# A first transformer with its own attention class: shifted rows by DMA, two scalings on ScalarE, query lengths on the score rows, narrow products in one run

## Chip, cores and metric

One core of one Trainium2 chip runs the whole program. The metric is the device time of one execution in microseconds (us); the time before is the median of three runs. TensorE (PE; its weight loads are shown as PEld), VectorE (DVE), ScalarE (ACT), GpSimd (POOL) and the queue of SyncE (SP), which issues most of the DMAs, each take their instructions in the order in which the program lists them. That order comes from a scheduler at build time, which places the instructions that the Python generators emit.

## The reference, cut to what matters

The program is a chain of four blocks on 4 x 512 tokens of width 128 (the kernel's layout), each an attention-like part times the SiLU of a feed-forward-like part. The change touches the "feed-forward" of the third block, which is itself a transformer of 6 layers with 16 heads of 64 and a window of 32:

```python
def shift_tokens(t):              # the second half of the columns comes from the token before
    a, s = jnp.split(t, 2, -1)
    s = jnp.pad(s, ((0, 0), (1, 0), (0, 0)))[:, :-1]
    return jnp.concatenate([a, s], -1)
def attn_layer(x, Wqkv, qs, ksc, Wo):
    q, k, v = heads of (x @ Wqkv)
    q = l2norm(q) * qs            # unit length, then a learned scale
    k = l2norm(k) * ksc
    q = q * cos * scale + rotate_half(q) * sin * scale
    k = k * cos * inv + rotate_half(k) * sin * inv
    ...
    sim = einsum('bhwie,bhwje->bhwij', bq, bk2) * 8.0     # own window and the one before, masked
    out = softmax(sim) @ bv2
    return out @ Wo
def ffn_layer(x, g, bln, W1, b1, W2, b2):
    xn = layernorm(x) * g + bln
    a, gate = jnp.split(xn @ W1 + b1, 2, -1)
    return a * gelu(gate) @ W2 + b2
for i in range(6):
    x = attn_layer(shift_tokens(x), ...) + x
    x = ffn_layer(shift_tokens(x), ...) + x
```

The fourth block has a second transformer (2 layers, 8 heads, window 64) that shares some of the code.

## The kernel before

`transformer` (L707) builds one `_Transformer` for each of the two and runs three generators side by side: `queries_keys`, `attention` and `feed_forward`. Work goes by rows (layer, batch entry), 24 of them in the first transformer, and each row has two slots (`gp`, eight heads each), so 48 slots. In a slot `merge` takes the next piece of the generator that is least far along; the `yield` values are the planned TensorE times. All TensorE results go through one pool of four PSUM tiles of two banks (`S2`, printed as S).

- `queries_keys` (L1278). The shifted row `hb` is made by two DVE copies and a memset (`shifted`, L84 to L91). For queries (i = 0), then keys (i = 1), two groups g: two 128x512 products into one S tile (projections `hb,l_wqk`), their squares on ACT (L1304), the two halves added on POOL (L1305), two products with the rotary table on DVE (L1306, L1308), their sum on POOL (L1309). `unit_length` (L1319) sums the squares over each head with two products against ones, takes Ln and Exp on ACT (L1329, L1330) and scales the rotated tile on DVE (L1333); eight DMAs (L1340) then stack it by heads into `l_qk`. `tables` (L1250) loads a rotary table by DMA once per layer and kind and scales it on DVE (L1258).
- `attention` (L1495). A unit is half a slot (`j`). `scores` (L1383): two masks as products with an identity, 64 narrow products (64 rows x 32 columns), the transposes of the last unit (`turn`, L1431) in their middle, then on DVE the row maxima (L1415), the subtraction in two halves (L1419), the exponential on ACT (L1424), the sums on DVE (L1426). `turn_back` (L1484) transposes the unit before that, `wo` is multiplied (L1532), the row `xn` updated (L1533). `weigh` (L1443): 64 narrow products of the last unit in two pieces, then the division on DVE (L1473). `values` (L1343): products 128x64 by 256 columns in two pieces, an eviction each (L1365), four DMAs into the buffer `l_ve` with the keys' windows one step on.
- `feed_forward` (L1543). Shift by DVE again, mean and variance by two products, the normalised row on DVE (L1558) and its gain and offset on DVE (L1559), three pairs of products with W1, GELU on ACT (L1569), the product on DVE (L1571), three with W2, the update (L1579). The second transformer runs the same function.

Of the kernel before, what the change touches and what calls it, by code (L numbers as in the profile page):

```python
# [38 lines left out]
class Net:  # L39
# [667 lines left out]
    def transformer(self, pre, depth, heads, window, consts):  # L707

        with ExitStack() as stack:
            pool = lambda name, bufs=1, **kw: stack.enter_context(self.pool(pre + name, bufs, **kw))
            pools = [pool("ps", 4, space=PSUM)]

            pools += [pool("c", side="right"), pool("tab", 3, side="right"), pool("w", side="right")]
            pools += [pool("qk", 4), pool("v", 2), pool("p", 2), pool("t", 2)]
            t = _Transformer(self, pre, heads, window, pools, consts)
            t.exp_tables()  # L720
            rows = [(l, b) for l in range(depth) for b in range(B)]
            passes = t.queries_keys(rows), t.attention(rows), t.feed_forward(rows)
            slots = len(rows) * t.GP
            for i in range(slots + t.GP + 2 + t.lag):
                run = []
                if i < slots:
                    run.append((until_none(passes[0]), 10.3))
                if 0 < i <= slots + 1 + t.lag:
                    run.append((until_none(passes[1]), t.attention_weight))
                if i >= t.GP + 2 + t.lag:  # L730
                    run.append((until_none(passes[2]), t.feed_forward_weights[i % t.GP]))
                merge(run)
# [448 lines left out]
class _Transformer:  # L1181
    def __init__(self, net, pre, heads, window, pools, consts):
        self.net, self.nc, self.a, self.pre = net, net.nc, net.a, pre
        self.heads, self.W, self.inner = heads, window, heads * 64
        self.GP = heads // 8
        self.NB = 128 // window
        self.split = self.NB == 4
        self.PS, C, self.TB, self.WT, self.QK, self.VP, self.PP, self.TP = pools
        nc, a = self.nc, self.a
        self.T = 4 if self.split else 2  # L1190
        self.NU = self.T * 64 // window
        self.cols = net.load(C, a[pre + "cols"], name=pre + "_cols")
        k = net.load(C, a[consts][:, 0:256], name=pre + "_k", queue=nc.scalar)
        self.ones, self.cen = k[:, 0:128], k[:, 128:256]
        self.tiny = C.tile([128, 1], F32, name=pre + "_tiny")
        nc.vector.memset(self.tiny, 1e-36)
        n = NT // self.T
        self.mask = C.tile([128, n, 512], BF16, name=pre + "_mask")
        nc.gpsimd.dma_start(self.mask, a[consts][:, 256 : 256 + 512 * n].rearrange("p (t n) -> p t n", t=n))
        self.identb = C.tile([128, 128], BF16, name=pre + "_identb")  # L1200
        nc.vector.tensor_copy(self.identb, net.ident)

        self.ve = [C.tile([128, self.NU, 1024 // self.NB], F32, name=f"{pre}_ve{i}") for i in range(2)]
        for i in range(2 if self.split else 1):
            for lo, hi in self.second():
                nc.gpsimd.memset(self.ve[i][lo:hi, 0, :], 0.0)
        self.made, self.shift, self.weights = {}, {}, {}

        self.attention_weight = 20.4 if self.split else 25.0
        self.feed_forward_weights = (7.7, 1.7) if self.GP == 2 else (9.4,)  # L1210


        self.lag = 1 if self.split else 0
        self.y = net.xn
# [104 lines left out]
    def unit_length(self, sums, t):  # L1319

        net, nc = self.net, self.nc
        p = self.S2()
        for g in range(2):
            net.mm(p[:, g, :], self.ones, sums[g][:, 0, :])
            if g or not self.split:
                yield 1.72 if self.split else 0.86
        nc.scalar.activation(p, p, AF.Ln, bias=self.tiny)  # L1329
        nc.scalar.activation(p, p, AF.Exp, scale=-0.5)  # L1330
        for g in range(2):

            nc.vector.scalar_tensor_tensor(  # L1333
                t[:, g], p[:, g, :].unsqueeze(1).to_broadcast([128, 2, S]), 1e12, t[:, g], ALU.min, ALU.mult
            )
        out = self.QK.tile([128, 2, 2, S], F32, name=self.pre + "_qk")
        for r in range(4):
            for h in range(2):
                x = 32 * (2 * (r % 2) + h)
                nc.sync.dma_start(out[x : x + 32, :, r // 2, :], t[32 * r : 32 * r + 32, :, h, :])  # L1340
        return out
# [201 lines left out]
    def feed_forward(self, rows):  # L1543
        net, nc = self.net, self.nc
        for l, b in rows:
            w1, w2 = self.ff_weights(l)
            yb = net.tok(self.y, b)
            hb = net.shifted(yb, self.TP, 3)
            p = self.S2()
            net.mm(p[:, 0, :], self.cen, hb)  # L1550
            sq = self.TP.tile([128, S], F32, name="ffg", bufs=1)
            nc.scalar.activation(sq, p[:, 0, :], AF.Square)
            yield 0.86
            net.mm(p[:, 1, :], net.mean, sq)
            rstd = self.TP.tile([128, S], F32, name="ffu", bufs=3)
            nc.scalar.activation(rstd, p[:, 1, :], AF.Ln, bias=net.eps)
            nc.scalar.activation(rstd, rstd, AF.Exp, scale=-0.5)
            nc.vector.tensor_tensor(hb, p[:, 0, :], rstd, ALU.mult)  # L1558
            nc.vector.tensor_scalar(hb, hb, self.col(l, 0), self.col(l, 1), ALU.mult, ALU.add)  # L1559
            yield 0.86  # L1560
            if self.GP == 2:
                yield None
            u = []
            for j, (k0, n) in enumerate(HID_TILES):
                p = self.S2()
                net.mm(p[0:n, 0, :], w1[:, k0 : k0 + n], hb)
                net.mm(p[0:n, 1, :], w1[:, HID + k0 : HID + k0 + n], hb)
                g = self.TP.tile([128, S], F32, name="ffg", bufs=1)
                nc.scalar.activation(g[0:n], p[0:n, 1, :], AF.Gelu, bias=self.col(l, 5 + j)[0:n])  # L1569
                u.append(self.TP.tile([128, S], F32, name="ffu", bufs=3))  # L1570
                nc.vector.scalar_tensor_tensor(  # L1571
                    u[j][0:n], p[0:n, 0, :], self.col(l, 2 + j)[0:n], g[0:n], ALU.add, ALU.mult
                )
            self.exp_tables()
            yield 5.2
            p = self.M()
            for j, (k0, n) in enumerate(HID_TILES):
                net.mm(p, w2[0:n, j, :], u[j][0:n], j == 0, j == 2)
            nc.vector.scalar_tensor_tensor(yb, p, self.col(l, 8), yb, ALU.add, ALU.add)  # L1579
            yield 2.6  # L1580
            yield None

def _constants():
# [19 lines left out]
    for name, t in (("l2", L2F), ("l3", L3F)):  # L1605
        w = t["window"]
        ones = np.kron(np.eye(4), np.ones((32, 32)))
        cen = np.eye(128) - 1.0 / 128

        block, i = np.arange(128) // w, np.arange(128)[:, None] % w  # L1610
        j = np.arange(w)[None]
        mask = np.zeros((128, NT, 2, 2, w), f)
        for q in range(NT):
            for blk in range(128 // w):
                rows = block == blk
                own, before = (0, 1) if blk % 2 == 0 else (1, 0)
                mask[rows, q, :, own] = np.where(j <= i, 0.0, MASKED)[rows][:, None]
                seen = (j >= i) & (q + blk > 0)
                mask[rows, q, :, before] = np.where(seen, 0.0, MASKED)[rows][:, None]
        c["k_" + name] = np.concatenate([ones, cen, mask.reshape(128, -1)], 1)  # L1620
        c["k_rot_" + name] = _rotary(w // 2, w)
    return {k: np.ascontiguousarray(v, dtype=f) for k, v in c.items()}
# [32 lines left out]
    return np.stack(out, 1)  # L1655


def _halves(w, heads, even_first):

# [3 lines left out]
    for g in range(heads // 4):  # L1665
        for i in range(2):
            for half in range(2):
                order.append((i * n + (4 * g + r) * 64 + 32 * half + d).reshape(-1))
    v = 2 * n + np.arange(n).reshape(heads // 8, 8, 64)
    for part in v:  # L1670
        order += [part[0::2].reshape(-1), part[1::2].reshape(-1)] if even_first else [part.reshape(-1)]
    return w[:, :, np.concatenate(order)]


def _layout(i):
# [19 lines left out]
    for pre, src, names in (  # L1695
# [2 lines left out]
    ):  # L1698
        for dst, n in zip(("Wqkv", "Wo", "W1", "W2"), names):
            a[pre + dst] = i[src + n]  # L1700
        a[pre + "Wqkv"] = _halves(a[pre + "Wqkv"], (L2F if pre == "l2" else L3F)["heads"], pre == "l2")
        a[pre + "cols"] = _columns(*(i[src + n] for n in ("q_scale", "k_scale", "ln_g", "ln_b", "b1", "b2")))
    a["L3_attn_A"] = i["L3_attn_A"]

# [22 lines left out]
```

## Time and profile before

| what | value |
|---|---|
| three runs | 3869.68, 3872.96, 3877.02 us; median 3872.96 us |
| span of the profiled execution, first to last instruction | 3866.4 us (its own time outside the span is not recorded; the median lies 6.6 us above the span) |
| TensorE, VectorE, ScalarE, GpSimd busy | 90%, 64%, 48%, 30% of the span |
| first transformer | about 1565 to 3270 us |
| second transformer | about 3400 us to the end |
| in 1565 to 1800 us | TensorE 206.0 busy of 235.0 us, granted clock 0.96 |
| in 3400 to 3867 us | TensorE 393.4 of 467.0 us, VectorE 315.6, granted clock 0.94 |

An engine's share is an average over stages; the stage that the change touches has its own rows. The granted clock is the share of full speed that TensorE was given. The groups of the profile give, for one engine and line, how often it ran, the busy time, the mean of one in ns, and the idle time just before with what ended it. Busy TensorE time is modelled at its ends, so its price is read from start to start in the timeline. A 128x512 product in fp32 is recorded as two instructions.

### The profile page before, as it was taken

The numbers are of one execution on the slowest core, as the hardware profiler recorded it, in microseconds if no ns is written. First come the engines' busy times: TensorE is split into PE (matmuls) and PEld (weight loads), VectorE is DVE, ScalarE is ACT, GpSimd is POOL, SyncE is SP. The second block draws the span as 40 slices with busy tenths as digits, with TensorE's granted clock in tenths as the row PEclk, the third lists the DMA queues.
The fourth block names the chain that finished last, engine by engine and source line by source line (L and its number), as shares of the span: only waits on it lengthen the run. The fifth ranks groups of instructions, "written<-read, shape, count | busy, mean of one in ns | idle before, by whom it ended". The sixth has DMA issues, their size and how long they took to land.

```text
span 3866.4 us, 105326 instructions
## 1 busy us (share of the span) xinstructions
PE 3490.9 (90%) x46789; PEld 1892.2 (49%) x46917; DVE 2476.9 (64%) x3429; ACT 1847.0 (48%) x2508; POOL 1161.2 (30%) x994
## 2 busy tenths in 40 slices
PE   6886999899899999899999999999999999778887
PEld 4554455444444443454555555555555555445444
DVE  6675555411553351677888888888888887367765
ACT  3333666623133334455555555555555555445555
POOL 1001344400021113443443443443443342042220
PEclk7677999999899999999999999999999999889998
DMA  1000000001000000444334444444444434322221
GB/s 39 8 24 24 8 1 1 1 30 52 2 1 3 3 1 2 116 99 117 95 94 122 96 96 120 95 99 117 98 99 103 103 88 98 110 63 69 53 49 42
DMA packets 123574, 236.12 MB, mean 61 GB/s; under 512 B 29624, under 2 KB 44128, under 8 KB 117728
## 3 DMA queue, kind: packets, MB, share of 16 engines
q1 hardware_dynamic: 114064, 209.58, 22.1%
q10 hardware_dynamic: 8624, 19.29, 1.6%
q8 instruction: 369, 6.05, 0.7%
q0 software_dynamic: 432, 0.51, 0.1%
q14 instruction: 85, 0.70, 0.1%
HBM read 50.08 MB, written 5.54 MB: 14 GB/s over the span
## 4 chain that ended last, share of the span: by engine, by line
PE 69%; ACT 11%; DVE 9%; issue 6%; DMA 2%; POOL 2%; SPq 0%; DVEq 0%; POOLq 0%; ACTq 0%
PE S L122 45%; PE S L126 6%; PE M L122 5%; PE S L1402 4%; PE o L1104 4%; ACT l_P L581 3%; PE o L614 2%; ACT l_PT L1440 1%; DMA l_tab<-in_k_rot_l 1%; PE S L1014 1%; DVE l_mx L1079 1%; ACT l_P L1126 1%; DVE l_rot L1333 1%; PE M L741 1%; DVE l_rot L1306 1%
## 5 line engine op out<-in xcount | busy, mean ns | idle before, releaser
L1309 POOL TENSOR_TENSOR l_rot<-l_rot,rotp 128x1024 f32<-128x1024 f32 x224 | 527.5, 2364 | 285.9 <-DVE rotp L1308 219.2
L1305 POOL TENSOR_TENSOR sqp<-sqp 128x512 f32<-128x512 f32 x224 | 293.3, 1310 | 832.8 <-ACT sqp L1304 825.6
L122 PE MATMUL S<-hb,l_wqk 128*128 128x512 f32 x896 | 449.4, 621 | 36.7 <-ACT l_PT L1440 11.2
L1304 ACT ACTIVATE sqp<-S 128x1024 f32<-128x1024 f32 x224 | 229.5, 1025 | 319.2 <-PE S L122 318.0
L1333 DVE SCALAR_TENSOR_TENSOR l_rot<-S,l_rot 128x1024 f32<-128x1024 f32 x224 | 262.9, 1211 | 65.3 <-ACT S L1330 37.4
L1306 DVE TENSOR_TENSOR l_rot<-S,l_tab 128x1024 f32<-128x1024 f32 x224 | 272.1, 1215 | 50.0 <-ACT sqp L1304 46.6
L126 PE MATMUL S<-core,l_P 128*128 128x128 f32 x1856 | 265.2, 287 | 38.9 <-ACT l_P L1424 16.4
L126 PEld LDWEIGHTS S<-core,l_P 128*128 128x128 f32 x1856 | 215.0, 146 | 136.8 <-issue 45.8
L122 PE MATMUL S<-l_KT,l_QT 32*128 32x256 f32 (+7 forms) x1536 | 247.4, 475 | 34.7 <-ACT l_P L1126 14.5
L1126 ACT ACTIVATE l_P<-S 128x1024 f32<-128x1024 f32 x160 | 156.8, 1023 | 254.9 <-PE S L122 254.1
L1308 DVE TENSOR_TENSOR rotp<-S,l_tab 128x1024 f32<-128x1024 f32 x224 | 270.5, 1208 | 1.4 <-POOL l_rot L1309 1.3
L122 PEld LDWEIGHTS S<-hb,l_wqk 128*128 128x128 f32 x896 | 158.3, 192 | 224.7 <-issue 151.6
L122 PE MATMUL S<-sqp,l_k 128*128 128x512 f32 x448 | 226.5, 623 | 19.1 <-issue 7.2
L1402 PE MATMUL S<-l_qk 64*32 64x64 f32 (+1 forms) x13312 | 221.1, 230 | 19.4 <-DMA l_qk<-l_rot 1.9
L1079 DVE TENSOR_REDUCE l_mx<-S 128x2 f32<-128x768 f32 (+1 forms) x192 | 154.9, 863 | 123.8 <-PE S L1014 123.8
L1402 PEld LDWEIGHTS S<-l_qk 64*32 64x32 f32 (+1 forms) x13312 | 168.2, 108 | 134.0 <-issue 129.6
L1130 POOL TENSOR_SCALAR_AFFINE_SELECT l_P<-l_P 128x256 f32<-128x256 f32 x256 | 99.8, 408 | 405.5 <-ACT l_P L1126 398.5
L122 PE MATMUL S<-l_wv,hb 128*64 128x256 f32 (+1 forms) x1600 | 219.1, 395 | 2.4 <-ACT l_vo L1365 1.2
L122 PE MATMUL S<-l_OT,l_wo 128*128 128x512 f32 (+1 forms) x512 | 207.1, 544 | 8.0 <-DVE ffu L1571 7.9
L1415 DVE TENSOR_REDUCE mx<-S 128x16 f32<-128x1024 f32 (+1 forms) x128 | 155.7, 1216 | 89.9 <-PE S L1402 89.8
L122 PE MATMUL S<-hb,l_w 128*128 128x512 f32 (+1 forms) x384 | 189.6, 630 | 23.5 <-DVE hb L1559 14.1
L122 PEld LDWEIGHTS S<-l_ve,l_PT 64*32 64x32 f32 (+1 forms) x6656 | 159.9, 108 | 99.2 <-issue 70.5
(360 smaller groups left out, 6544.8 us busy)
## 6 DMA issues: line engine op xcount, KB each, us to landing
l_qk<-l_rot SPq DMA_DIRECT2D x896, 128.0 KB
l_ve<-l_vo SPq DMA_DIRECT2D x112, 256.0 KB
l_ve<-l_vo SPq DMA_DIRECT2D x96, 224.0 KB
l_tab<-in_k_rot_l ACTq DMA_DIRECT2D x16, 1024.0 KB
l_wqk<-in_l2Wqkv SPq DMA_DIRECT2D x12, 512.0 KB
l_wv<-in_l2Wqkv SPq DMA_DIRECT2D x12, 256.0 KB
l_wo<-in_l2Wo SPq DMA_DIRECT2D x12, 256.0 KB
l_ve<-l_vo SPq DMA_DIRECT2D x24, 128.0 KB
```

Source lines behind the costliest of these rows:

```text
L122: self.nc.tensor.matmul(out, lhsT, rhs, start=start, stop=stop)
L126: self.nc.tensor.transpose(out, in_, self.ident[:n, :n])
L1079: nc.vector.tensor_reduce(mxv[:, bs, 2 * m + e, 3 - i], s[u][:, :, c : c + n], axis=AX.X, op=ALU.max)
L1126: nc.scalar.activation(P[u], s[u], AF.Exp, scale=scale)
L1304: nc.scalar.activation(sq, p, AF.Square)
L1305: nc.gpsimd.tensor_tensor(sq[:, 0, :], sq[:, 0, :], sq[:, 1, :], ALU.add)
L1306: nc.vector.tensor_tensor(t[:, g], p, tab[:, 0], ALU.mult)
L1308: nc.vector.tensor_tensor(m, p, tab[:, 1], ALU.mult)
L1309: nc.gpsimd.tensor_tensor(t[:, g], t[:, g], m[:, ::-1, :], ALU.add)
L1333: nc.vector.scalar_tensor_tensor(t[:, g], p[:, g, :].unsqueeze(1).to_broadcast([128, 2, S]), 1e12, t[:, g], ALU.min, ALU.mult)
L1402: net.nc.tensor.matmul(sv[W * bl : W * bl + W, e, t, g, :].rearrange("p (s k) -> p s k", s=2), qk[0][r, g, j, W * c : W * c + W], kw, star ...
L1415: nc.vector.tensor_reduce(mx, flat, axis=AX.X, op=ALU.max)
```

## The change

`_Paired`, a subclass with its own `queries_keys`, `values`, `scores`, `weigh`, `turn_back` and `attention`, takes the place of `_Transformer` where the window is 32. What it does:

- `moved` builds the shifted row by two DMAs on SP's queue. For the projections it is issued at the second slot of the row before, for the feed-forward as soon as the attention's last update of the row is emitted.
- `tables` scales the rotary tables on ACT. Keys come before queries. Only keys go through `unit_length`; for queries `lengths` sums the squares by 32 products of 32 x 4 outputs, takes Ln and Exp of 128x32 and clips on POOL. The resulting factor is multiplied to the score rows after the maximum is subtracted, by a POOL instruction between the subtraction and the exponential.
- `scores` of a unit and `weigh` of the last one are emitted with no piece between them. The subtraction is one instruction instead of two; `turn_back` has one eviction instead of two; the update of `xn` is two instead of one.
- `values` takes 128x512 products (four per slot) instead of 16 of 128x64 by 256, and its output layout changes with the weights' order on the host; `P`, `PT` and `On` have one buffer.
- In `feed_forward`, for both transformers, gain and offset move from DVE to ACT. The masks and the planned attention weight (20.4 to 16.1) follow.

```diff
-            t = _Transformer(self, pre, heads, window, pools, consts)
+            t = (_Paired if window == 32 else _Transformer)(self, pre, heads, window, pools, consts)
...
-        self.attention_weight = 20.4 if self.split else 25.0
+        self.attention_weight = 16.1 if self.split else 25.0
...
-            hb = net.shifted(yb, self.TP, 3)
+            hb = self.shift.pop(("ff", l, b)) if self.split else net.shifted(yb, self.TP, 3)
...
-            nc.vector.tensor_scalar(hb, hb, self.col(l, 0), self.col(l, 1), ALU.mult, ALU.add)
+            nc.scalar.activation(hb, hb, AF.Identity, bias=self.col(l, 1), scale=self.col(l, 0))
...
+    def moved(self, b, tag):
+        y = self.net.tok(self.y, b)
+        hb = self.TP.tile([128, S], F32, name=tag, bufs=2)
+        nc.gpsimd.memset(hb[64:128, 0:1], 0.0)
+        nc.sync.dma_start(hb[0:64, :], y[0:64, :])
+        nc.sync.dma_start(hb[64:128, 1:S], y[64:128, 0 : S - 1])
+        return hb
+    def tables(self, l, i):
...
+                nc.scalar.mul(v, v, self.col(l, 9 + 2 * i + h))
...
+    def queries_keys(self, rows):
...
+                if gp and n + 1 < len(rows):
+                    self.shift[rows[n + 1]] = self.moved(rows[n + 1][1], "hb")
+                before, made = None, {}
+                for i in (1, 0):
...
+                        if before:
+                            made["k"] = yield from self.unit_length(*before)
+                            before = None
+                    before = sums, t
+                made["q"] = self.stack(t)
+                made["r"] = yield from self.lengths(sums)
...
+    def lengths(self, sums):
+        p = self.M()[:, 0:32]
+        pv = p.rearrange("p (h n) -> p h n", h=4)
+        for t in range(2):
+            for g in range(2):
+                for a in range(2):
+                    for bl in range(4):
+                        c = 4 * (2 * t + bl // 2) + 2 * a + bl % 2
+                        net.mm(
+                            pv[32 * bl : 32 * bl + 32, :, 4 * t + 2 * g + a], sums[g][:, 0, 32 * c : 32 * c + 32], self.ones[:, ::32]
+                        )
+        yield 0.8
+        r = net.stat(32, "rq")
+        nc.scalar.activation(r, p, AF.Ln, bias=self.tiny)
+        nc.scalar.activation(r, r, AF.Exp, scale=-0.5)
+        nc.gpsimd.tensor_scalar(r, r, 1e12, None, ALU.min)
+        return r
...
+    def weights_of(self, u, s, r):
+        mx = net.stat(16, "mx")
+        sv = s.rearrange("p e (n k) -> p (e n) k", k=64)
+        nc.vector.tensor_reduce(mx, sv, axis=AX.X, op=ALU.max)
+        P = u["P"] = self.PP.tile([128, 16, 64], F32, name=self.pre + "_P", bufs=1)
+        nc.vector.tensor_tensor(P, sv, mx.unsqueeze(2).to_broadcast([128, 16, 64]), ALU.subtract)
+        rq = r[:, 16 * u["j"] : 16 * u["j"] + 16]
+        nc.gpsimd.tensor_tensor(P, P, rq.unsqueeze(2).to_broadcast([128, 16, 64]), ALU.mult)
+    def exponentials(self, u):
+        self.nc.scalar.activation(u["P"], u["P"], AF.Exp, scale=8.0)
+    def turn(self, u):
...
+        u["PT"] = self.PP.tile([128, 8, 128], F32, name=self.pre + "_PT", bufs=1)
+        nc.scalar.copy(u["PT"], t)
+        rs = net.stat(16, "rs")
+        nc.vector.tensor_reduce(rs, P, axis=AX.X, op=ALU.add)
+        u["r"] = net.stat(16, "r")
+        nc.vector.reciprocal(u["r"], rs)
+    def close(self, u, OT):
...
+        for t in range(2):
+            nc.vector.tensor_tensor(y[:, t], y[:, t], p[:, t], ALU.add)
+        if u["gp"]:
+            self.shift["ff", u["l"], u["b"]] = self.moved(u["b"], "fb")
+    def attention(self, rows):
...
+        for i in range(len(units) + 2):
+            if i % 2:
+                yield None
...
+                s = self.scores(qk, u["j"])
+            if last:
+                o = self.weigh(last)
+            if u:
+                self.weights_of(u, s, qk["r"])
+            if last:
+                self.divide(last, o)
+            if u or last:
+                yield 2.8
+            behind = None
+            if i % 2 == 0 and i + 2 < len(units):
+                behind = self.values(units[i + 2])
+            elif i % 2 and i > 2:
+                behind = self.close(units[i - 2], OT.pop(i - 2))
+            if behind:
+                yield next(behind)
+            if u:
+                self.exponentials(u)
+            if behind:
+                yield from behind
+            if last:
...
+                self.turn_back(last, made)
+                yield 0.9
+            if u:
+                self.turn(u)
+                yield 0.9
```

The built program lists TensorE's work of a typical row of the changed kernel as four units, each from the end of one unit's scores to the end of the next one's; every unit begins with `weigh` of the last unit and ends with two masks and the scores:

```
A: weigh | cen, projection, wo, projection, mean, transposes back, transposes, masks, scores
B: weigh | key sums, projection, values, values, lengths, transposes back, transposes, projection, masks, scores
C: weigh | three W1 pairs, projection, wo, projection, transposes back, transposes, masks, scores
D: weigh | key sums, projection, values, W2, values, lengths, transposes back, transposes, projection, masks, scores
```

In the same listing VectorE has, from one row maximum to the next, in unit B of one row (q0, q1: the two table products of a projection)

```
maximum, q1, subtraction, two divisions, sum, two unit lengths, q0, q1, reciprocal
```

and ScalarE `exponential, Exp of the key lengths, square, two value evictions, Ln and Exp of the query lengths, two transposed evictions, square`; in the next row's unit B the Ln of the key lengths stands behind the exponential too, and the first q1 behind the divisions.

## The prediction

> **What bounds the kernel now.** I read the table of stretches first, then the groups of each engine in 1800 to 3000 us, where the first transformer runs steadily, then TensorE's timeline, start to start. The stretch:
>
> ```profile
> core 0: us, PE busy (x) PEld busy (x) DVE busy (x) ACT busy (x) POOL busy (x), PEclk, DMA share, GB/s
> 1800.00:3000.00 1200.00, 1146.15 (x20719) 633.56 (x20785) 999.57 (x1083) 646.25 (x732) 494.15 (x302) 1.00 0.43 105
> ```
>
> TensorE is busy 95.5% at full clock; VectorE 83%. Groups of that stretch (busy, mean ns of one, idle before; the L595 row is from the whole program):
>
> ```profile
> L122 PE MATMUL S<-hb,l_wqk 128*128 128x512 f32 x532 | 259.4, 610 | 14.2 <-ACT l_PT L1440 7.6 <-ACT l_OT L1493 4.8 <-DVE rotp L1308 1.6
> L122 PE MATMUL S<-sqp,l_k 128*128 128x512 f32 x268 | 132.4, 616 | 6.6 <-issue 5.5 <-POOL sqp L1305 0.8
> L1333 DVE SCALAR_TENSOR_TENSOR l_rot<-S,l_rot 128x1024 f32<-128x1024 f32 x133 | 155.6, 1211 | 22.4 <-ACT S L1330 20.7
> L89 DVE COPY hb<-xn 64x512 f32<-64x512 f32 x33 | 51.9, 1573 | 0.6
> L1559 DVE TENSOR_SCALAR hb<-hb,l_cols 128x512 f32<-128x512 f32 x17 | 39.7, 2334 | 0.6
> L90 DVE COPY hb<-xn 64x511 f32<-64x511 f32 x33 | 30.6, 929 | 0.7
> L1329 ACT ACTIVATE S<-S,l_tiny 128x1024 f32<-128x1024 f32 x67 | 72.5, 1082 | 56.1 <-PE S L122 54.4 <-DVE rotp L1308 0.9 <-DVE l_tab L1258 0.9
> L1309 POOL TENSOR_TENSOR l_rot<-l_rot,rotp 128x1024 f32<-128x1024 f32 x135 | 317.9, 2365 | 172.6 <-DVE rotp L1308 125.1 <-DMA l_ve<-l_vo 47.6
> L595 POOL TENSOR_TENSOR l_P<-l_P,l_r 128x1024 f32<-128x1024 f32 x48 | 90.9, 1895 | 66.6 <-DVE l_r L586 56.0 <-PE S L126 10.6
> ```
>
> 532 projections at 16 a slot are 33.25 slots, so a slot takes 36.09 us; idle TensorE is (1200 - 1146)/33.25 = 1.6 us of it. What bounds is TensorE's work and the changes between its shapes, with VectorE (30.1 us a slot) close behind. Prices, by the start of the next group:
>
> ```profile
> 2303.86 1.88 PE L122 MATMUL S<-hb,l_wqk 128*128 128x512 f32 x4
> ...
> 2307.08 1.95 PE L122 MATMUL S<-l_wv,hb 128*64 128x256 f32 x16
> 2308.95 1.98 PE L122 MATMUL S<-sqp,l_k 128*128 128x512 f32 x4
> 2310.78 0.38 PE L122 MATMUL S<-l_mask,l_identb 128*128 128x512 bf16 x1
> 2311.30 0.86 PE L1402 MATMUL S<-l_qk 64*32 64x64 f32 x64
> 2312.09 1.09 PE L126 MATMUL S<-core,l_P 128*128 128x128 f32 x8
> 2313.02 1.88 PE L122 MATMUL S<-hb,l_wqk 128*128 128x512 f32 x4
> ```
>
> Half a 128x512 product costs 0.43 us (4 in 1.72), a values piece 1.87, masks 0.52, half the scores 0.79, eight transposes 0.93; the two halves of `weigh`, 2305.66 to 2307.08, cost 1.42.
>
> **The change on TensorE.** Before, a slot is: projections 16 x 0.43 = 6.9, sums of squares 8 x 0.43 = 3.4, values 3.7, wo 3.4, feed-forward 11 x 0.43 = 4.7 (22 halves a row), transposes 3.7, masks 1.0, scores 3.2, `weigh` 2.8: 33.0. The change takes 4 halves of query sums (-1.72) and makes values 8 x 0.43 = 3.44 (-0.3). `lengths` adds 64 recorded instructions of 128x32 weights. The same shape, with 18 columns, ran 12.7 ns apart in the first stage (early `l_vo` and `l_ve` products); tiny 32x32 products there ran up to 28 ns apart. So 64 x 12.7 ns = 0.8 us; bounds 0.7 (`weigh`'s 1.42 for 128) and 1.8. Scores and `weigh` in one run: eight narrow runs a slot become two, and `lengths` a third; a run costs about 0.1 us going in (2303.86 to 2305.66 is 1.80 for four halves, not 1.72) and 0.13 coming out, so 5 x 0.23 = 1.1 less. Work and crossings fall by 1.7 + 0.3 - 0.8 + 1.1 = 2.3 us a slot.
>
> **On the other engines, per slot.** VectorE loses two L1333 (2.4), the shifts (82.5/33.25 = 2.5), L1559 (1.2) and the tables (0.5): 30.1 to about 23.5. ScalarE loses one Ln and Exp pair (2.1), gains two of 128x32 at 0.19, half a 0.65 affine, two table scalings of 1.05 per table: 19.4 to about 18.5. GpSimd gains two multiplications of 128x1024 by a broadcast factor: L595 is that form, 1.90; the upper bound is L1309, 2.36. 14.9 to 18.7. SP gains two DMAs a slot, with 20 there at 0.64 us each (14 of 36 us). The row for the next projections is issued one slot early, so its transfer is covered; if that cover were gone a 1 MB table took 5 us from issue to use, a 128 KB row less. Moving the feed-forward row puts a wait for the update of `xn` on SP; behind it stand the next stack of `l_qk`, which is used about 18 us later. None of this is on the path. The update and subtraction splits are worth 0.1.
>
> **What the change puts on the path.** The exponential now waits for the GpSimd multiplication, and VectorE's row sum, ScalarE's lengths, squares and evictions stand behind it in order. I walked a row through the program's order, unit by unit, with these prices: end of products to a reader 0.26, between engines 0.06, VectorE 1.21 (1.13 apart when independent, as in the two rows below), ScalarE 1.02 (0.94 apart), GpSimd 1.90, 1.31 and 2.36.
>
> ```profile
> 2317.20 1.21 DVE L1415 TENSOR_REDUCE mx<-S 128x16 f32<-128x1024 f32 x1
> 2318.33 1.22 DVE L1308 TENSOR_TENSOR rotp<-S,l_tab 128x1024 f32<-128x1024 f32 x1
> ```
>
> From the end of the scores: maximum 1.46, subtraction 2.7, multiplication 4.7, exponential 5.8.
> - B, one row: the maximum stands behind the normalised row and a table product (1.4 to 2.6), the subtraction ends at 4.9; on GpSimd a 2.36 rotation sum, waiting for q1 at 3.75, ends at 6.2, the multiplication at 8.1. Exponential 9.2, Exp of key lengths 10.15, square 11.1, GpSimd's add 12.5. TensorE reaches `lengths` at 9.0 (1.45 + 1.72 + 0.6 wait + 1.72 + 3.44) and waits 3.6. Unit 19.3 us. In the next row the order is kinder: multiplication at 4.7, `lengths` free at 10.2, wait 1.6; 17.0.
> - C: exponential 5.8, table load 1.28, GELU 0.69, product 0.75: the first W1 tile is free at 8.6, TensorE there at 6.6. Wait 2.0; 19.6.
> - A: one row waits 0.45 only (14.6). In the next the row sum stands ahead of the key projection's table products: 5.8, sum 7.1, reciprocal, q0, q1 at 9.5, TensorE there at 7.9; with 0.75 for the normalised row, 16.9.
> - D: 17.7 and 18.15.
>
> Two rows: 71.2 and 71.65, so 35.7 us a slot. The same prices, with the waits that the trace shows, give 36.4 for the slot before, 1% long; so 35.4 to 35.7, I take 35.55. Gain 0.54 x 48 = 26 us. So growing waits eat some three quarters of the 2.3 us that the work loses.
>
> Three small terms. L1559 in the second transformer's 8 rows: 2.33 becomes 0.65; from 0 to 8 x 1.68 = 13 us, I take -5, as VectorE there is busy only 315.6 of 467 us. Tables on ScalarE: the scaling waits for its DMA,
>
> ```profile
> 2397.24 0.75 DVE L1258 TENSOR_SCALAR l_tab<-l_tab,l_cols 128x1024 f32<-128x1024 f32 x1 [2.26 <-DMA l_tab<-in_k_rot_l]
> ```
>
> and holds ScalarE's queue (exponential, evictions) instead of VectorE's: 0 to 2.3 us more for each of ten tables, +4 taken. The clock, in TensorE's timeline and the table of stretches:
>
> ```profile
> 2402.08 2.83 PE L122 MATMUL S<-hb,l_w 128*128 128x512 f32 x4 [2.53 <-DVE l_rot L1333]
> ```
>
> ```profile
> 2403.50:2410.20 6.70, 6.28 (x80) 3.13 (x79) 2.18 (x3) 2.81 (x4) 0.09 (x1) 0.78 0.75 176
> ```
>
> TensorE waited 2.53 us and the granted clock fell to a mean of 0.78 in the next 6.7 us; the four halves took 2.83 instead of 1.98. So a wait of 2.5 us or more can cost some 0.85 to 1.7 us. The 3.6 us wait of B comes in every second row: 12 times, about half of them, 1.3 us: +8; from 0 to 41 (two in each of 24 rows).
>
> [...]
>
> Sum, against the profiled span of 3866.4: -26 - 5 + 4 + 8 = -19, 3847; the median lies 6.6 above the span: **3854 us**.
>
> **Rivals.**
> 1. TensorE's work decides and the waits stay at 1.6 us, because B's and C's queues run ahead in the steady state: 36.09 - 2.3 = 33.8 a slot, 48 x 2.3 = 110 less, 3763. For it: VectorE falls to 65%. Against it: the order within each queue is fixed.
> 2. Slower: the GpSimd link. At L1309's price the multiplication takes 0.46 more; four units a row, 24 rows: 45 us; waits in B and C then pass 2.5 us and the clock falls twice a row, 33 us more than taken. 3854 + 45 + 33 = 3932. It decides from about 2.1 us a multiplication: 96 of them spend the 19 us at 0.2 us each. For it: TensorE idles in every unit by my walk. Against it: L595 is the nearer form.
> 3. The change doesn't do what it says: the shifted rows arrive late because SP waits for `xn`, or queries wait for `l_qk`. About 2 us in each of 24 rows: 3900. Against it: 22 DMAs of 0.64 us keep SP's queue busy 14 of 36 us.
>
> **How the numbers follow.** Forecast 0.40, its own range 3825 to 3885; rival 1 0.22; rival 2 0.28; rival 3 0.06; nothing told by a measurement 0.04. 0.2% (8 us, about what three runs tell from no change) is 3865 to 3881: the forecast case gives 0.29 faster, 0.08 same, 0.03 slower; with the rivals faster 0.51, same 0.12, slower 0.37. The range reaches rival 1's price and rival 2's: 3765 to 3935.
>
> **What would show it.** Right: L1333 halved and no L89, L90 in the first transformer; `lengths` near 0.8 us; slots near 35.5 us with TensorE idle 3 us of them, ended by VectorE and ScalarE in B and C; the multiplication near 1.9 us; short falls of the clock in 1800 to 3000 us. Wrong: idle TensorE still near 1.6 us a slot (rival 1), a multiplication of 2.3 us or waits that start at GpSimd in every unit (rival 2), TensorE waiting for DMAs of `hb`, `fb` or `l_qk` (rival 3).

## The result, and the profile after

Timed beside each other, the changed kernel takes 4120.15 us (median of four runs, 4112.57 to 4128.63) and the kernel before 3874.99 us (3869.68 to 3883.64): a ratio of 1.063, 95% interval 1.0605 to 1.0663. The profiled execution of the changed kernel spans 4117.5 us, 251 more than the one before. The forecast was 3854, so it was wrong in sign and by 266 us.

The loss lies in the first transformer. From the start of slot 10 to that of slot 47 (found in the timeline by counting 16 projections a slot) a slot takes 41.24 us; before it took 35.99. The tables of stretches of the kernel before and of the changed one, in this order (columns as in the table of the prediction):

```profile
1900.00:3100.00 1200.00, 1149.37 (x20726) 635.77 (x20771) 1001.55 (x1084) 646.57 (x734) 494.48 (x302) 1.00 0.42 103
1900.00:3100.00 1200.00, 983.51 (x19173) 568.34 (x19216) 705.41 (x777) 532.43 (x610) 540.84 (x350) 0.93 0.41 96
```

TensorE is busy 82% of it where it was busy 96%, at a granted clock of 0.93 instead of 1.00. The other engines did what was forecast: per slot (465 projections at 16 a slot are 29.06 slots) VectorE 24.3 us, ScalarE 18.3, GpSimd 18.6. The groups of that stretch of the changed kernel say where TensorE stood:

```profile
L122 PE MATMUL S<-hb,l_wqk 128*128 128x512 f32 x465 | 230.5, 619 | 61.3 <-issue 59.3 <-DVE rotp L1645 1.7 <-DVE ffu L1575 0.2
...
L1722 POOL TENSOR_TENSOR l_P<-l_P,rq 128x1024 f32<-128x1024 f32 x59 | 112.2, 1901 | 87.0 <-DVE l_P L1720 84.4 <-PE S L122 2.3
...
L122 PE MATMUL S<-l_ve,l_PT 64*32 64x64 f32 x3768 | 107.2, 232 | 52.8 <-issue 52.8
...
L122 PE MATMUL S<-l_vo,l_PT 64*32 64x64 f32 x3770 | 104.7, 233 | 60.6 <-issue 60.6
L1708 PE MATMUL S<-l_qk 64*32 64x64 f32 x7424 | 92.2, 227 | 22.7 <-issue 14.6
...
L1333 DVE SCALAR_TENSOR_TENSOR l_rot<-S,l_rot 128x1024 f32<-128x1024 f32 x58 | 68.2, 1217 | 36.1 <-ACT S L1330 36.1
```

Read the last column. `weigh` (`l_ve`, `l_vo`) and the scores (L1708) have 136 us of idle time just before them, 4.7 us a slot, nearly all put down to "issue": the profile shows nothing that they waited for. In the kernel before the two `weigh` groups had 1.7 us in the same stretch:

```profile
L122 PE MATMUL S<-l_vo,l_PT 64*32 64x64 f32 x4288 | 106.9, 225 | 1.4 <-issue 1.3
L122 PE MATMUL S<-l_ve,l_PT 64*32 64x64 f32 x4288 | 104.6, 224 | 0.3 <-issue 0.2
```

The projections of the changed kernel have 61.3 us, nearly all in three waits. L1333 is halved and the multiplication on GpSimd takes 1901 ns, as forecast.

**The waits inside the narrow runs.** TensorE's timeline of the changed kernel, around one of them:

```profile
2134.73 1.58 PE L1708 MATMUL S<-l_qk 64*32 64x64 f32 x128
2136.11 0.34 PE L122 MATMUL S<-l_ve,l_PT 64*32 64x64 f32 x3
...
2136.71 0.21 PE L122 MATMUL S<-l_vo,l_PT 64*32 64x64 f32 x1
2139.47 0.24 PE L122 MATMUL S<-l_vo,l_PT 64*32 64x64 f32 x1 [2.54 <-issue]
```

and the queues in the DMA view of 2136.70 to 2139.50 us (packets, MB, share of 16 engines):

```profile
q8 instruction: 1, 0.02, 2.1%
```

The wait falls in the middle of `weigh`, between products that read the same tiles, so their operands should all have been there. In it lies one packet of a DMA queue called "instruction". Over the whole program that queue moved 384 packets of 16 KB for 97,162 recorded TensorE instructions, one for every 253. Put in a list, the 103 waits over 0.5 us in narrow runs between 1600 and 3520 us (222 us in all) stand, but for three, a multiple of 256 recorded instructions apart, semaphore instructions counted (511 or 767 where a record is missing), and 95 of them hold such a packet. In the median TensorE goes on 2.6 us after the packet starts, and the packet starts 1.1 us after the first instruction of the 256 before. So by an estimate from these two medians 256 instructions gone through in less than about 3.7 us leave TensorE without instructions. That a packet brings the next 256 is the author's reading of these counts; no view shows what is in a packet. The spacing of the packets says nearly the same without the waits: in the traces of the kernel before and of the changed one no two packets of that queue start less than 3.3 us apart, while the 128 products and 128 loads of the scores above were through in 1.38 us (2134.73 to 2136.11). A unit's scores and `weigh`, 256 recorded products and as many weight loads, are 512 instructions in about 3 us (1.38 for the scores, 1.42 for `weigh` in the prediction); in the kernel before, runs of narrow products were 64 long or shorter, and 128 once a slot.

**The waits at a layer's first projection.** SP's queue and TensorE, from their timelines in the changed kernel:

```profile
2154.55 0.50 SPq L1600 DMA_DIRECT2D hb<-xn  x1
2155.09 0.60 SPq L1601 DMA_DIRECT2D hb<-xn  x1
2165.99 13.62 SPq L1344 DMA_DIRECT2D l_qk<-l_rot  x16
...
2182.65 0.61 SPq L1239 DMA_DIRECT2D l_wqk<-in_l2Wqkv  x1
```

```profile
2167.11 1.04 PE L126 MATMUL S<-core,l_P 128*128 128x128 f32 x8
2187.62 3.75 PE L122 MATMUL S<-hb,l_wqk 128*128 128x512 f32 x4 [19.47 <-issue]
```

The load of the next layer's weights (L1239) stands on SP behind 16 DMAs of `l_qk`, and these wait for the last rotation of the layer. In 1900 to 3100 us this is the longest item of SP's own waits (total, times, longest):

```profile
SPq L1344 <- DVE l_rot L1333: 478.2, 29, 24.4
```

The load is issued at 2182.65; TensorE wanted it at 2168. In the kernel before the same load was issued at 2083.89, 22 us ahead of its first use at 2106.33, behind an earlier stack:

```profile
2064.49 19.30 SPq L1340 DMA_DIRECT2D l_qk<-l_rot  x16
2083.89 0.54 SPq L1239 DMA_DIRECT2D l_wqk<-in_l2Wqkv  x1
```

The changed kernel has five such waits, 97 us in all. The label "issue" stands here as well, so the cause has to be read from SP's queue.

### The profile page after: what moved, and what is told of

The parts are those of the page before. It is cut to its first block, busy times and chain, and to the rows that moved or that the text cites. A ratio compares the mean times of both kernels' runs of the same rounds, so it can differ in the third digit from the quotient of the medians.

```text
span 4117.5 us, 108849 instructions
## 1 busy us (share of the span) xinstructions
PE 3471.0 (84%) x48517; PEld 1920.0 (47%) x48645; DVE 2202.6 (53%) x3133; ACT 1800.5 (44%) x2468; POOL 1343.1 (33%) x1136
## 4 chain that ended last, share of the span: by engine, by line
PE 61%; issue 11%; ACT 10%; DVE 9%; DMA 3%; POOL 3%; SPq 3%; DVEq 0%; POOLq 0%; ACTq 0%
PE S L122 38%; PE S L126 5%; PE M L122 5%; PE o L1104 3%; PE S L1708 3%; ACT l_P L581 3%; SPq L1344 2%; PE o L614 2%; PE S L1014 1%; DVE l_mx L1079 1%; ACT l_P L1126 1%; DMA l_tab<-in_k_rot_l 1%; ACT sqp L1641 1%; POOL l_P L1722 1%; PE S L1406 1%
## 5 line engine op out<-in xcount | busy, mean ns | idle before, releaser
L1646 POOL TENSOR_TENSOR l_rot<-l_rot,rotp 128x1024 f32<-128x1024 f32 x192 | 451.7, 2359 | 236.6 <-DVE rotp L1645 230.1
L1642 POOL TENSOR_TENSOR sqp<-sqp 128x512 f32<-128x512 f32 x192 | 244.4, 1273 | 529.7 <-ACT sqp L1641 520.4
L1643 DVE TENSOR_TENSOR l_rot<-S,l_tab 128x1024 f32<-128x1024 f32 x192 | 233.8, 1218 | 203.6 <-ACT sqp L1641 197.1
L122 PE MATMUL S<-l_ve,l_PT 64*32 64x64 f32 (+1 forms) x6656 | 212.7, 231 | 95.3 <-issue 92.1
L122 PE MATMUL S<-l_vo,l_PT 64*32 64x64 f32 (+1 forms) x6656 | 209.5, 232 | 81.4 <-issue 81.4
L1725 ACT ACTIVATE l_P<-l_P 128x1024 f32<-128x1024 f32 x96 | 101.3, 1055 | 394.6 <-POOL l_P L1722 389.2
L1718 DVE TENSOR_REDUCE mx<-S 128x16 f32<-128x1024 f32 x96 | 117.4, 1223 | 272.1 <-PE S L1708 272.0
L1722 POOL TENSOR_TENSOR l_P<-l_P,rq 128x1024 f32<-128x1024 f32 x96 | 182.5, 1901 | 152.5 <-DVE l_P L1720 147.2
L122 PE MATMUL S<-l_wv,hb 128*128 128x512 f32 x448 | 210.3, 600 | 4.9 <-DVE l_rot L1333 2.8
L122 PEld LDWEIGHTS S<-l_vo,l_PT 64*32 64x32 f32 (+1 forms) x6656 | 170.5, 110 | 92.3 <-issue 92.1
```

The lines of the kernel that those rows point to most:

```text
L122: self.nc.tensor.matmul(out, lhsT, rhs, start=start, stop=stop)
L1642: nc.gpsimd.tensor_tensor(sq[:, 0, :], sq[:, 0, :], sq[:, 1, :], ALU.add)
L1643: nc.vector.tensor_tensor(t[:, g], p, tab[:, 0], ALU.mult)
L1646: nc.gpsimd.tensor_tensor(t[:, g], t[:, g], m[:, ::-1, :], ALU.add)
L1722: nc.gpsimd.tensor_tensor(P, P, rq.unsqueeze(2).to_broadcast([128, 16, 64]), ALU.mult)
```

## The experiments

All ratios are against the kernel before, run beside it. "Slot" is the mean from slot 10 to slot 47, "waits" those over 0.5 us in narrow runs of the first transformer, whatever ended them.

| kernel | median us | ratio (95%) | slot us | waits (us) |
|---|---|---|---|---|
| changed | 4120.15 | 1.0634 (1.0605 to 1.0663) | 41.24 | 103 (222) |
| e12 before, narrow runs joined | 4020.98 | 1.0392 (1.0361 to 1.0423) | 39.10 | 119 (200) |
| e1 narrow runs parted | 3957.17 | 1.0219 (1.0188 to 1.0250) | 37.38 | 59 (78) |
| e2 weights early | 4064.70 | 1.0510 (1.0471 to 1.0549) | 39.95 | 103 (223) |
| e8 rows on VectorE | 4080.21 | 1.0528 (1.0488 to 1.0568) | 40.35 | 99 (219) |
| e3 parted, weights early | 3933.77 | 1.0162 (1.0134 to 1.0190) | 36.79 | 62 (80) |
| e4 e3, values' weights early | 3865.36 | 0.9983 (0.9964 to 1.0001) | 35.14 | 65 (80) |
| e6 e4, multiplication on VectorE | 3867.32 | 0.9985 (0.9969 to 1.0002) | 35.42 | 55 (74) |
| e5 e4 in halves | 3956.44 | 1.0221 (1.0203 to 1.0239) | 37.28 | 30 (50) |
| e7 e4, `weigh` first | 3875.16 | 1.0001 (0.9984 to 1.0017) | 35.80 | 50 (66) |
| e9 e7, spread | 3907.25 | 1.0084 (1.0063 to 1.0105) | 36.01 | 54 (86) |
| e11 e4, GELUs together | 3854.74 | 0.9950 (0.9933 to 0.9966) | 34.97 | 67 (76) |
| e10 e11, GELU buffer, `wo` early | 3825.59 | 0.9878 (0.9857 to 0.9900) | 34.41 | 57 (77) |

### Is it the joined run?

e1 takes the joined run out of the changed kernel:

```diff
                 s = self.scores(qk, u["j"])
+                self.weights_of(u, s, qk["r"])
+                yield 1.4
             if last:
                 o = self.weigh(last)
-            if u:
-                self.weights_of(u, s, qk["r"])
-            if last:
                 self.divide(last, o)
-            if u or last:
-                yield 2.8
+                yield 1.4
```

> The scores and `weigh` of a unit get their pieces back (1.4 us each), so that the merge puts a wide product between them; nothing else changes, and every operand comes from where it came. Theory 1 (instructions arrive late): in the changed kernel 103 waits of about 2.15 us inside these narrow runs, 222 us in all, stand a multiple of 256 recorded TensorE instructions apart and 95 of them go with a 16 KB packet of an instruction queue. With 256 recorded instructions between wide products instead of 512 most of them go, as in the kernel before (4 waits, 5 us): 120 to 215 us less, 3905 to 4000. Rival (an operand is late, the transposed weights or the values from DMA): the waits stay, within 20 us of 4120.

It is 163 us faster than the changed kernel, with 59 waits where there were 103; 46 of the 59 (62 us) still stand a multiple of 256 apart, and most of the others wait for the squares on GpSimd. e12 puts the joined run into the kernel before and leaves all else (GpSimd, the rows, the scalings, the query sums) as it was: the two sets of transposes go ahead of the scores, and the `yield`s inside scores and `weigh` go (the diff is shortened).

```diff
+            if self.split:
+                if older: self.turn_back(older, OT)
+                if last: yield from self.turn(last)
             ...
-                u["P"], u["r"] = yield from self.scores(qk, u["tp"], u["j"], last)
+                u["P"], u["r"] = yield from self.scores(qk, u["tp"], u["j"], None)
+            if self.split:
+                if last: yield from self.weigh(last)
+                yield 4.88
```

> The kernel before, with one part of the change alone: the transposes of a unit first, then its scores and `weigh` in one run of 128 + 128 products with no piece between. All other work, tiles and engines as before. Theory (late instructions): 96 such runs of 512 recorded instructions, each with about one wait of 2.2 us: +200 us, less up to 0.23 us for each of five changes of shape a slot that go (48 slots, 55 us), 4000 to 4090, with waits of a multiple of 256 recorded instructions apart, labelled as waiting for nothing. Rival (joined narrow runs are no loss in themselves, the waits in the changed kernel came with its GpSimd link, its DMAs or its lengths): 3810 to 3890.

Its groups in 1900 to 3100 us:

```profile
L122 PE MATMUL S<-l_vo,l_PT 64*32 64x64 f32 x3951 | 108.6, 229 | 49.8 <-issue 49.8
L122 PE MATMUL S<-l_ve,l_PT 64*32 64x64 f32 x3952 | 107.8, 229 | 65.0 <-issue 51.1 <-ACT l_PT L1438 13.9
```

It is 155 us slower than the kernel before it ran beside, with 101 us of idle time put down to "issue" in these two groups, in 30.5 slots (488 projections / 16). Of the 119 waits in its first transformer 95 (174 us) again stand 256 or a multiple apart; of the other 24 (26 us) 22 wait for the transposed weights (`l_PT`). So this one edit costs about 3.1 us a slot (39.10 - 35.99), and the 101 us labelled "issue" are 3.3 us a slot. The rival, that the waits came with the GpSimd link, the DMAs or the lengths, is out: this kernel has none of these changes.

### The weights

e2 asks for the two projection weights of the next layer half a row earlier, ahead of the row's DMAs; e4 does so for the values' weights too (the second argument pair):

```diff
                 if gp and n + 1 < len(rows):
+                    self.part("qk", rows[n + 1][0], 0), self.part("v", rows[n + 1][0], 0)
                     self.shift[rows[n + 1]] = self.moved(rows[n + 1][1], "hb")
+                if n:
+                    self.part("qk", l, 1), self.part("v", l, 1)
```

> The two query and key weights of the next layer are asked for half a row earlier, ahead of the shifted row's DMAs; nothing else changes. Theory 2 (weights late): the five waits of 18 to 20 us at the layers' first projection, 97 us in all, are for `l_wqk`, whose DMAs stand on SP behind 16 DMAs of `l_qk` that wait for the last rotation. They go: 4015 to 4040. Rival (the shifted row or the update it waits for is late): they stay, 4110 to 4130, and TensorE waits for `hb`.

The five waits are gone, and the waits in narrow runs are as many as before (103), but the gain is 55 us, not 80 to 105. TensorE's waits in this kernel, 1900 to 3100 us (total, times, longest), show the next load in line:

```profile
PE S L122 <- issue: 121.3, 62, 5.6
PE S L122 <- DMA l_wv<-in_l2Wqkv: 34.2, 3, 11.8
```

> Both edits. If the two losses are separate: 120 to 215 and 80 to 100 us less than 4120, 3805 to 3920. If one hides behind the other (the stream of instructions is late because of what SP's queue does): about what the better one gives alone, 3900 to 4040.

e3 lies 186 us below the changed kernel, where e1 and e2 alone gained 163 and 55. That is 14 us short of the range for two separate losses and inside the range of the rival, so the time alone does not decide. The traces do: e1 still has all five waits for the projections' weights (14 to 19 us each), e2 still has the waits in narrow runs, and e3 has neither the five waits nor more than 62 in narrow runs. The losses are separate; what keeps the gain small is the same wait for `l_wv`, some 11 us in each of five layers, which takes the place of the five.

> The version with both edits, and the values' weights asked for early as well. In the version with both edits TensorE still waits five times some 9 us at a layer's first values product, 43.7 us of them in 1900 to 3100 us for the DMA of `l_wv`. If the queue is the cause: 40 to 55 less than 3934, 3880 to 3895. If the values' product only takes over another wait there (its eviction or the shifted row): within 15 us of 3934.

e4 takes 68 us off e3, more than expected; the granted clock of 1900 to 3100 us rose from 0.96 to 0.99 with it:

```profile
1900.00:3100.00 1200.00, 1124.10 (x22679) 636.18 (x22677) 818.22 (x906) 674.97 (x753) 636.58 (x413) 0.99 0.48 114
```

It stands level with the kernel before (0.9983, 0.9964 to 1.0001).

Which part of the change put the loads there? e8 puts both shifted rows back on VectorE in the changed kernel:

> The changed kernel with both shifted rows copied by VectorE at their use again, as in the kernel before; the rest of the change stays. If the rows' DMAs in SP's queue are what moves the weights' loads behind the stacks of `l_qk`: from the third layer on the loads stand early again, four of the five 19 us waits go, and the waits for instructions stay: 4030 to 4065. If the loads are late for another reason: 4100 to 4140, the 2.5 us a slot on VectorE being covered.

It gained 40 us, short of the range. The first of the two loads is early again in it, and the wait has moved to the second:

```profile
PE S L122 <- issue: 121.6, 60, 5.0
PE S L122 <- DMA l_wqk<-in_l2Wqkv: 44.5, 3, 15.0
```

So the rows' DMAs are part of the cause, not the whole. The place of a load in SP's queue is chosen at build time; what else in the change moves the second load back stays open. That asking earlier mends it is shown.

### The link over GpSimd

> As the version with early values, with the multiplication of the scores by the query lengths on VectorE (1.2 us) instead of GpSimd (1.90). If the link over GpSimd holds TensorE (the rival of the forecast, waits that start there): each of 96 exponentials comes 0.7 us earlier, 20 to 65 us less than the version before it. If TensorE does not wait for it: within 10 us of that version, or some 10 slower as VectorE's queue grows by 2.4 us a slot.

`nc.gpsimd.tensor_tensor` became `nc.vector.tensor_tensor` in `weights_of`. No difference: 3867.32 and 3865.36, and in 1900 to 3100 us no wait of TensorE in e4 names the multiplication. TensorE does not wait for it once the five long waits are gone and the narrow runs are parted.

### Is there more to gain?

e5 parts the runs further, into halves of 64 products with the merge weights of the kernel before (`yield 1.24`, `yield 1.2`, 20.3):

> As the version before it, with scores and `weigh` in halves of 64 products, the merge's weights as in the kernel before (1.24, 1.2, 20.3). The 62 waits (80 us) left in narrow runs should go if they are waits for instructions: 30 to 75 us less than the version before it, 3815 to 3860. Against it works the older cost that the forecast named, 0.23 us for each further change of shape, up to four a unit here: 96 units x 0.5 to 0.9 us = 45 to 90 us. If that holds and few waits go: 3890 to 3950.

The waits for instructions fell to 30 (50 us), yet it is 91 us slower than e4. In their place TensorE waits for buffers that are held longer (1900 to 3100 us, the four items behind "issue"):

```profile
PE S L122 <- DVE l_P L1724: 23.4, 33, 1.4
PE S L122 <- DVE ffu L1575: 22.1, 18, 2.9
PE S L122 <- DVE rotp L1648: 16.3, 6, 3.3
PE S L122 <- DVE l_On L1768: 10.4, 5, 2.3
```

These are part of the 2.1 us a slot by which e5 is slower than e4 (37.28 against 35.14); how much the further changes of shape cost was not taken apart. In e4 the longest item of that list is another one, and ScalarE's groups explain it:

```profile
PE S L122 <- DVE ffu L1575: 26.1, 12, 3.3
PE S L122 <- issue: 21.9, 27, 1.9
```

```profile
L1573 ACT ACT_TABLE_LOAD x36 | 46.2, 1283 | 0.6
...
L1728 ACT ACT_TABLE_LOAD x18 | 23.1, 1283 | 0.3
...
L1276 ACT ACT_TABLE_LOAD x17 | 21.8, 1283 | 0.3
```

Parting the run let the exponential (L1728) slip between two GELUs of a row, with four table loads a row instead of two. e7 moves `weigh` ahead of the scores in every second unit, so that the GELUs stand first:

> As the version with early values, with `weigh` ahead of the scores in every second unit, so that the three GELUs of a row stand together and ahead of the exponential on ScalarE. In the version with early values the exponential falls between the GELUs: three table loads of 1.28 us a row instead of two there and one more going back, and TensorE waits 34.5 us in 17 rows (2 us each) for the buffer of the first product of W1. If ScalarE's tables hold TensorE: about 2 us x 24 rows = 48 less, some of it taken back by new waits, 3815 to 3850. If that buffer is held by something else: 3855 to 3880.

The loads fell to two a row and the buffer wait went, but the time did not: waits for instructions moved into the scores (24.2 us), 19.3 us went to the DMA of `l_wo` and 14.7 to the exponential. e9 spreads the runs further and asks for `wo` early:

> As the version with `weigh` first in every second unit, with two products of values and one projection standing between scores and `weigh` in the other units (0.9 us of wide products before, 4.3 to 7 now), and the weights of `wo` asked for two slots earlier. In that version 50 waits of 1.3 us are left in narrow runs (66 us), and TensorE waits 19.3 us for the DMA of `l_wo` in 1900 to 3100 us. If the theory of late instructions holds, a third to two thirds of the waits go (20 to 45 us), and the wait for `l_wo` goes (25 us over the stage): 3875 - 45 to 70, 3805 to 3830. If a buffer or the exponential holds TensorE in their place: 3850 to 3880.

It got worse, and the theory failed here in its detail: 54 waits (86 us) are left, 52 of them a multiple of 256 apart, although 5 us and more of wide products stand between most of the runs. In about a fifth of them the 256 instructions before had taken 5 us and more, and the packet still started late, some 2.5 us before TensorE went on. What else delays a packet was not found.

e11 keeps e4's order on TensorE and only queues the exponential behind the row's last GELU:

```diff
+            with self.net.tc.issue_after(self.gelu.ins):
                 self.nc.scalar.activation(u["P"], u["P"], AF.Exp, scale=8.0)
```

> As the version with early values, with the exponential queued behind the row's last GELU and nothing else. If the tables are the whole of it: as the run with three edits, 3815 to 3845; if the single GELU buffer delays the third GELU and so the exponential: 10 to 25 more than that run; if tables do not matter: 3855 to 3875.

> As the version with early values, whose order on TensorE is kept (no order of scores and `weigh` is changed), with three edits beside it: the exponential is queued behind the row's last GELU, the GELU tile has two buffers instead of one, and the weights of `wo` are asked for two slots earlier. In the version with early values ScalarE loads tables 71 times in 1900 to 3100 us (1.28 us each, four a row) against 33 before, and TensorE waits 34.5 us there in 17 rows for a buffer behind them. If that is what holds: 2 us x 24 rows = 48 less at most, 3815 to 3845. If the exponential, now later by a GELU, holds the transposes instead, as in the version with `weigh` first: 3860 to 3880.

e11 halves the table loads (35 where e4 has 71) and takes the wait for L1575 from 26.1 to 3.6 us in the stretch, but gains only 11 us on e4 (0.9950 against 0.9983, their intervals just touch), far from the 48 at most that were expected: the tables are a small part. `l_wo` is what TensorE waits for next (11.5 us in the stretch). e10 adds a second GELU buffer and asks for `wo` two slots earlier (`self.part("o", l, 1 - gp)` in `queries_keys`): 3825.59 us, faster than the kernel before by 1.2% (0.9857 to 0.9900). Which of the two edits gave the 29 us against e11 was not taken apart. Its stretch:

```profile
1900.00:3100.00 1200.00, 1130.44 (x22991) 647.80 (x23060) 835.73 (x928) 641.10 (x731) 649.75 (x421) 1.00 0.48 115
```

The clock is back at 1.00 and 558/16 = 34.9 slots fit where the changed kernel had 29.06 and the kernel before 33.5.

## Why the prediction was wrong

- **The step that failed first** was the fourth term of the work sum: "a run costs about 0.1 us going in [...] and 0.13 coming out, so 5 x 0.23 = 1.1 less". The forecast put a gain of 1.1 us a slot there. Alone, in the kernel before, joining the runs costs 3.1 us a slot (e12). The 0.23 was a price of changing shape, and no row priced what it stood against: what a run of 256 recorded products costs TensorE. No narrow run of the kernel before was longer than 128 recorded products, so its trace held no row for 256. But its page lists a queue called "instruction" (369 packets of 16 KB), and dividing the instructions by the packets would have asked the question.
- **The second** was "SP gains two DMAs a slot [...] None of this is on the path", and rival 3, "About 2 us in each of 24 rows", at a chance of 0.06. The mechanism was there, with another victim and another size: not the row and not `l_qk`, but the layer's weights, 18 to 20 us five times. The argument against it, "SP's queue busy 14 of 36 us", was the wrong measure. It counts what SP issues and not what it waits for: in 1900 to 3100 us SP waited 478 us for rotations alone (the longest 24.4), and the load of the weights that stood behind one was issued at 2182.65 us where TensorE wanted it at 2168. (In the kernel before it waited as long, 267 us for rotations and 339 us for evictions of the values, but there the loads stood behind an earlier stack.) I priced the DMAs by their number and looked at what stood behind the moved rows, but not at where the build would put the loads that were there before.
- **The clock** was forecast at +8 us, from 0 to 41. The records of the granted clock in 1900 to 3100 us show 171 us at half speed in the changed kernel (31 falls, of which three, 58 us, go with the long waits) and 3.4 us before; with the long waits gone and the runs parted (e4) they show 20.5 us, so most of it came with the two losses.
- **What held, and what agreed by luck.** With the long waits gone and the runs parted (e4) the kernel takes 3865 us; forecast were 3854. A slot takes 35.14 us, forecast 35.55. But e4 has runs of 128 products, not of 256, and its terms are not those of the forecast: TensorE's busy time fell by 1.3 us a slot (34.3 to 33.0), not by 2.3 (1.9 at the forecast's own prices for four narrow runs instead of two), and its idle time rose from 1.5 to 2.2 us, not by 1.8. Of that idle time 1.0 us is put down to "issue", which the forecast did not have; the wait of 1.6 to 3.6 us that the walk put ahead of `lengths` in unit B is 5.6 us in 17 rows, at most 1.2 in one; only the wait of unit C for a W1 tile is near its size (26.1 us in 17 rows, 1.5 in each, forecast 2.0). So the walk's waits were too long and its saving too large, and the two errors made up for each other. Prices that held, in the changed kernel: the multiplication took 1.90 us, the 64 instructions of `lengths` 0.65 to the next group where the sum had 0.8, and VectorE, ScalarE and GpSimd lie within 0.8 us a slot of the forecast. The -5 us for L1559 did not show: from slot 48 to the end it is 465.2 us before and 468.0 in e4. The tables' +4 was not tried alone.
- **Rival 1** (3763, waits stay small): e10 reaches 34.41 us a slot, not 33.8, with 77 us of waits left; that these are all of the difference was not shown. **Rival 2** (the GpSimd link, 3932) gave a time on the right side for a reason that e6 rules out; its condition, 2.1 us a multiplication, was not met either (1.90).
- **The range** of 3765 to 3935 took its upper end from rival 2 and left out a joint failure of two steps that had each been put at nothing or at a gain.

## What to carry to other kernels

Ask of every stretch not only what its operations cost, but how many instructions it takes a microsecond: some 500 in 3 us went with 103 waits of TensorE here, 256 between wide products still with 50 to 67, and the kernel before, with mostly 128, had four such waits. When DMAs are added to a queue that waits (SP here for 478 of 1200 us), look up in the built order where the loads of weights now stand, and ask for them early in the program. When a loss is mended, list the waits again: e2, e4 and e11 here each showed the next wait in line.

## What the runs showed of the hardware

- In the changed kernel TensorE stood still 103 times for more than 0.5 us in narrow runs of the first transformer, by 2.2 us in the median from start to start; all but three of these waits stand a multiple of 256 recorded instructions apart, and 95 go with a 16 KB packet of the queue "instruction", which moved one for every 253 recorded instructions of TensorE. That a packet brings a block of 256, and that a block gone through faster than the next one comes stops TensorE, is the author's reading: joining the runs in the kernel before (e12) took the waits from 4 to 119, parting them in the changed one (e1) from 103 to 59, and about a fifth of those in e9 do not fit it. The packets start at least 3.3 us apart in the traces of the kernel before and of the changed one, while weight loads and products of 64x32 follow each other some 5.4 ns apart (256 in 1.38 us of scores).
- In 1900 to 3100 us the granted clock fell to half speed for 3.4 us or a multiple: once for 3.4 us in the kernel before, 31 times for 3.4 to 20.5 us in the changed one. A wait of some 2.5 us was followed by a fall in one place and not in another: after the 2.53 us ahead of 2402.08 us in the kernel before there was one from 2403.0 us, after the 2.54 us ahead of 2139.47 us in the changed one the clock stayed at 1.00 to 2150 us. The kernel before with its runs joined (e12), whose longest wait at its products is 2.6 us, had 15 falls in 1900 to 3100 us. Which waits bring a fall stays open.
